# Two attentions of one layer on shared buffers, the second one's first pairs prepared beside the first one's last chunks

## The chip, the cores and the metric

The kernel runs on one core of a Trainium2 chip. The metric is the device time of one launch in microseconds (us). The kernel before took 2742.89 us in the median of three runs (2742.8 to 2744.47).

The engines have short names: PE multiplies matrices (PEld is its weight load), DVE, ACT and POOL work element by element, SP issues transfers. PE writes to PSUM[...]; POOL does not touch PSUM here, so DVE and ACT carry results out of it.

## What is computed

A small vision transformer on 128 images: a convolutional tokenizer makes 64 tokens of 256 features per image, then come two layers. The change concerns the first layer, whose two parts are added to the stream `h` one after the other:

```python
# h = h + A(layernorm(h)), per image, G = 8 groups of 32 features
diff = Qg - Kg                                   # every query with every key
attn = relu(einsum('bqkgd,d->bqkg', relu(diff), w_mlp) + b_mlp)
out  = einsum('bqkg,bkdg->bqdg', softmax(attn, axis=2), Vg)
# h = h + B(layernorm(h)), 4 slices of 64 features, E = 4 experts of 2 heads
xn   = normalized(x) * norm_w                    # x is the layernorm of h
gate = softmax(xn @ router_w.T + router_b)
y    = softmax(q @ k.T * scale) @ v              # per slice, expert and head
y    = y @ proj_w.T + proj_b
out  = x + (sum over experts of y * gate) @ out_w.T
```

A is called relu attention here, B expert attention. The second layer (a linear attention and a mixture of experts) follows and is the same in both kernels. All data are float32.

## The kernel before, in words

The stream stays in SBUF as `h2`, 64 rows of two images each, from the tokenizer to the end of expert attention. Both attentions write the order of the work on all engines out by hand: each engine runs its instructions in the order of the program, so a step that waits holds up all that stands behind it on its engine.

**Relu attention** (`relu_attention`, L290) takes 8 blocks of 16 images, and each block in 8 chunks of 8 query tokens: 64 chunks. In a chunk the maxima or differences of every query and key are formed on DVE (`larger`, L517), on POOL with a relu on ACT (`difference`, L525 and L526), and on ACT alone (`by_query`, L535). PE adds them up (`add`, L327). One chunk later come the softmax (`less_max` L551 to L553, `exponents` L558, `sums` L561, `weights` L565) and the transposes to `at` (L574, L582). The next block's statistics, normalization, transposes, keys and values are spread over the chunks through a table: `at(n, place, step)` puts a step into chunk `n` at one of the places O, X, A, V1, Y, B, W, V2, C, Z, in this order through the chunk. A finished block's sum with the values (`outcome`, L471), its copies (L482), the transposes back (`back`, L489) and the addition to the stream (`added`, L499) stand in chunks 9 to 11 after the block's first. After chunk 63 the last chunk's softmax, the last block's outcome and its addition follow alone; five matmuls without use (L49, `busy`) stand on PE meanwhile.

**Expert attention** (`expert_attention`, L774) opens its own pools after that. It loads its weights, multiplies the value weights with the projection (L806) and the projection's bias with the output weights (L819, `b4`, laid out as `bn`). It works in 16 blocks of 4 rows, called pairs as a row holds two images. A block's steps are the statistics (L843, L844, DVE), `factors` (nine POOL instructions with two powers, L852 to L860), `normal` (POOL: `xn` L866 and the stream with its residual L869), `transpose` and `transposed` (L874, L879), the logits of the router (L885) and their softmax, the gates (L892 to L904), and the gates transposed into `gT` (L908 on PE, L911 on ACT). For the first two blocks and part of the third these steps stand ahead of the first pair (`do("first")`); for the others they are spread over the pairs by a table like the first.

A pair has queries and keys (L933, copied by ACT L937), values (L945: two calls, one for each half of the features; the copies L954 stand on ACT for the first and on DVE for the second), scores (L965), softmax in two halves (L977, L978, L981, L984, L985, and on POOL L991 and L992, which puts the gates into the weights), transposes (L1001, copied by ACT L1004), the sum with the values (`mixed`, L1014, L1022) and the output (L1028). The bias comes in with one more matmul of the transposed gates (L1029), and L1030 adds the result to the stream. Pair p + 1's queries, keys and values and pair p - 1's transposes, sum and output are worked on between pair p's steps.

In PSUM relu attention has 2 banks for sums, 2 for queries, a ring of 3 and one bank for the softmax's transposes; expert attention has 4 banks for scores and a ring of 4.

Of the kernel before, what the change touches and what calls it, by code (L numbers as in the profile page):

```python
# [1 line left out]

# [287 lines left out]
def relu_attention(c, wqkv, wmlp, bmlp):  # L290
# [7 lines left out]
    NP = NB // 2  # L298
    with (
        tc.tile_pool(name="aw", bufs=1) as wp,  # L300
        tc.tile_pool(name="an", bufs=2) as np_,
        tc.tile_pool(name="ab", bufs=2) as bp,
        tc.tile_pool(name="aat", bufs=1) as atp,
# [3 lines left out]
        tc.tile_pool(name="ae", bufs=2) as ep,  # L307
        tc.tile_pool(name="aps", bufs=2, space=PSUM) as pss,
        tc.tile_pool(name="apc", bufs=2, space=PSUM) as psc,
        tc.tile_pool(name="apq", bufs=3, space=PSUM) as psq,  # L310
        tc.tile_pool(name="apt", bufs=1, space=PSUM) as pst,
    ):
        w = wp.tile([P, 2, 3 * D], F32, name="w")
# [21 lines left out]
        class Block:  # L335
# [41 lines left out]
            def transpose(self, i):  # L377

                if i == 0:
                    self.xT = bp.tile([P, 2, NP, P], F32, tag="xT", name="xT")  # L380
                self.ps["x", i] = pt = psq.tile([P, 2, 2, P], F32, tag="pq", name="pt")
                for fc in range(2):
                    for n in range(2):
                        nc.tensor.transpose(
                            pt[:, fc, n], self.xn[:, 2 * i + n, fc * P : fc * P + P], c.ident
                        )
# [5 lines left out]
            def keys(self, s, fo):  # L392

                self.ps["k", s, fo] = pk = psq.tile([P, 8, T], F32, tag="pq", name="pk")
# [15 lines left out]
            def values(self, i):  # L410

                self.ps["v", i] = pv = psq.tile([P, 2, D], F32, tag="pq", name="pv")
# [15 lines left out]
            def key_sums(self):  # L428
                self.ps["b"] = pk = psq.tile([P, T], F32, tag="pq", name="pkb")
# [34 lines left out]
            def outcome(self, hf):  # L464
                self.ps["o", hf] = po = [psq.tile([P, NP, T], F32, tag="pq", name="po") for _ in range(2)]
# [18 lines left out]
            def back(self, i):  # L484

                self.ps["h", i] = pt = psq.tile([P, 2, D], F32, tag="pq", name="pto")
# [14 lines left out]
        class Chunk:  # L501
# [65 lines left out]
            def transpose(self):  # L567


                self.pt = pt = pst.tile([P, 8, 64], F32, tag="pt", name="pt")  # L570
# [50 lines left out]
        for b, x in enumerate(blocks):  # L621
            n = 8 * b

            at(n + 9, "X", of(x.outcome, 0))
            at(n + 9, "A", of(x.outcome_copied, 0, 0))
            at(n + 9, "B", of(x.outcome_copied, 0, 1))
            at(n + 9, "Y", of(x.outcome, 1))
            at(n + 9, "C", of(x.outcome_copied, 1, 0))
            at(n + 10, "O", of(x.outcome_copied, 1, 1))
            for i in range(4):  # L630
                at(n + 10 + i // 2, "XY"[i % 2], of(x.back, i))
                at(n + 10 + (i + 1) // 2, ("V2", "V1")[i % 2], of(x.added, i))
# [48 lines left out]
            at(n, "B", of(x.valued, 3))  # L681

# [4 lines left out]
        with tc.manual_schedule():  # L687
# [61 lines left out]
            old.exponents()  # L749
            old.sums()  # L750
            old.weights()
            c.busy(psq.tile([P, 8, T], F32, tag="pq", name="idle"), blocks[-1].k[:, 0, 0:8], 5)
            old.transpose()
            old.transposed()
            for n in range(len(seq), len(seq) + 12):
                for place in ("O", "X", "A", "V1", "Y", "B", "V2", "C", "Z"):
                    do(n, place)
        assert not work


def expert_attention(c, hd, normw, wr, br, wqkv, wvT, wproj, bproj, wout):
# [7 lines left out]
    with (  # L769
        tc.tile_pool(name="fw", bufs=1) as wp,  # L770
        tc.tile_pool(name="fb", bufs=3) as bp,
        tc.tile_pool(name="fn", bufs=2) as np_,
        tc.tile_pool(name="fv", bufs=3) as vp,
        tc.tile_pool(name="fe", bufs=4) as ep,  # L774
        tc.tile_pool(name="fps", bufs=2, space=PSUM) as pss,
        tc.tile_pool(name="fpq", bufs=4, space=PSUM) as psq,
    ):
        nw = wp.tile([P, 2], F32, name="nw")
        nc.sync.dma_start(nw, normw)
        wrs = wp.tile([P, 2, 4], F32, name="wrs")  # L780
        nc.sync.dma_start(wrs, wr.rearrange("(c p) e -> p c e", p=P))
        brs = wp.tile([P, 4], F32, name="brs")
        nc.sync.dma_start(brs, br.partition_broadcast(P))
        w = wp.tile([P, 2 * D], F32, name="w")
        bp2 = wp.tile([P, 4], F32, name="bp2")
        for k in range(2):
            nc.sync.dma_start(w[k * 64 : k * 64 + 64, :], wqkv)
            nc.sync.dma_start(bp2[k * 64 : k * 64 + 64, :], bproj)
        wv = wp.tile([32, 8, 64], F32, name="wv")
        nc.scalar.dma_start(wv, wvT)  # L790
        wpj = wp.tile([32, 8, 64], F32, name="wpj")
        nc.scalar.dma_start(wpj, wproj)
        wo = wp.tile([P, 2, D], F32, name="wo")
        nc.scalar.dma_start(wo, wout.rearrange("(c p) n -> p c n", p=P))
        eps = wp.tile([P, NB], F32, name="eps")
        nc.gpsimd.memset(eps, LN_EPS)
        one = wp.tile([P, NB], F32, name="one")
        nc.gpsimd.memset(one, 1.0)


        pv = psq.tile([P, 2, D], F32, tag="pq", name="pwv")
        for k in range(2):
            for e in range(4):
                for h in range(2):
                    r = (e % 2 * 2 + h) * 64
                    nc.tensor.matmul(  # L806
                        pv[k * 64 : k * 64 + 64, e // 2, r : r + 64],
                        wv[:, e * 2 + h, :],
                        wpj[:, e * 2 + h, :],
                        start=True,  # L810
                        stop=True,
                    )
        wvp = wp.tile([P, 2, D], F32, name="wvp")
        nc.vector.tensor_copy(wvp, pv)


        pb = psq.tile([4, D], F32, tag="pq", name="pb")
        for fc in range(2):
            nc.tensor.matmul(pb, bp2, wo[:, fc, :], start=(fc == 0), stop=(fc == 1))  # L819
        b4 = wp.tile([4, D], F32, name="b4")  # L820
        nc.vector.tensor_copy(b4, pb)
        bn = wp.tile([P, NB, D], F32, name="bn")
        nc.gpsimd.memset(bn, 0.0)
        for n in range(NB):
            nc.sync.dma_start(bn[4 * n : 4 * n + 4, n, :], b4)
        gTs = [wp.tile([P, P], F32, name=f"gT{k}") for k in range(3)]
        for gT in gTs:
            nc.gpsimd.memset(gT, 0.0)

        class Block:  # L830
# [4 lines left out]
            def __init__(self, p0):  # L835
                self.p0, self.gT = p0, gTs[p0 // NB % 3]

            def statistics(self, n0):
                if n0 == 0:
                    self.mv = np_.tile([P, NB, 2], F32, tag="mv", name="mv")  # L840
                    self.st = np_.tile([P, NB, 6], F32, tag="st", name="st")
# [20 lines left out]
            def normal(self, n):  # L862
                if n == 0:
                    self.xn = np_.tile([P, NB, D], F32, tag="xn", name="xn")
# [199 lines left out]
        def do(key):  # L1064
            for step in work.pop(key, ()):
                step()
# [989 lines left out]
```

## Time and profile before

| | us |
|---|---|
| median of three runs | 2742.89 |
| the profiled execution's own time | 2744.63 |
| its span, first to last instruction | 2742.5 |
| PE, DVE, ACT, POOL busy in the span | 2598.4, 2027.9, 1623.1, 1633.7 |

The span has a tokenizer until about 181 us, relu attention until about 1098 us with its drain until 1114, expert attention until about 1941, and the second layer after that. The page's 40 slices show these stages (each slice is 68.6 us; a digit is the busy share in tenths):

```profile
PE   7989999999999999799999999999699986999997
DVE  5759999999998989477777777777467776444443
ACT  2228888888888888366656666666355543233332
POOL 3328888888888889656566656553233212454444
PEclk9999999999999999899999999999899998999998
```

The dip in the 17th slice is the change from one attention to the other. PEclk is the share of its clock that TensorE was granted. A busy PE is modelled from pipelined matmuls, so 9 on PE does not say that it is at its peak.

### The profile page before, as it was taken

What the parts mean: (1) busy time and instruction counts of PE and PEld (TensorE: products, weight loads), DVE (VectorE), ACT (ScalarE), POOL (GpSimd) and SP (SyncE); (2) the same over time, 40 slices, a digit from 0 to 9 for tenths busy, and PEclk for the clock granted to TensorE, in tenths of its full rate; (3) what the DMA queues carried; (4) which work ended last, traced back from release to release, by engine and by line L of the source; (5) the groups of instructions that cost most, each with busy time, mean ns of one, the idle gap of its engine ahead of it and who ended that gap; (6) DMA issues with size and microseconds to landing.
All of it is one profiled execution on the core that took longest, in us unless ns stands there. A gap on an engine that the chain in (4) does not pass through costs nothing. (4 is left out here: it accounts for less than half of the span.)

```text
span 2742.5 us, 77026 instructions
## 1 busy us (share of the span) xinstructions
PE 2598.4 (95%) x33309; PEld 1733.3 (63%) x33309; DVE 2027.9 (74%) x3025; ACT 1623.1 (59%) x3414; POOL 1633.7 (60%) x1390
## 2 busy tenths in 40 slices
PE   7989999999999999799999999999699986999997
PEld 4553444444344443588888888888466565888886
DVE  5759999999998989477777777777467776444443
ACT  2228888888888888366656666666355543233332
POOL 3328888888888889656566656553233212454444
PEclk9999999999999999899999999999899998999998
DMA  3000000000000000000000000000333454555554
GB/s 109 32 12 1 2 1 2 2 2 2 1 2 1 2 2 1 12 11 19 11 11 19 11 11 18 11 12 17 96 83 85 100 118 149 179 198 197 184 195 134
DMA packets 138015, 140.83 MB, mean 51 GB/s; under 512 B 107747, under 2 KB 121461, under 8 KB 129984
## 3 DMA queue, kind: packets, MB, share of 16 engines
q1 hardware_dynamic: 126928, 117.95, 14.2%
q0 software_dynamic: 7648, 14.77, 1.7%
q8 instruction: 263, 4.31, 0.6%
q10 hardware_dynamic: 3088, 3.08, 0.4%
q14 instruction: 88, 0.72, 0.1%
HBM read 103.96 MB, written 32.54 MB: 50 GB/s over the span
## 5 line engine op out<-in xcount | busy, mean ns | idle before, releaser
L525 POOL TENSOR_TENSOR m<-q,k 128x1024 f32<-128x1024 f32 x384 | 719.0, 1904 | 31.7 <-PE sc L327 16.3
L517 DVE TENSOR_TENSOR m<-pc,k 128x2048 f32<-128x2048 f32 (+1 forms) x320 | 646.7, 2058 | 0.5 <-ACT q L461 0.5
L327 PE MATMUL sc<-m,wide 128*32 128x512 f32 x4096 | 529.7, 599 | 12.0 <-DVE m L517 7.1
L526 ACT ACTIVATE m<-m 128x1024 f32<-128x1024 f32 x384 | 402.5, 1050 | 5.9 <-POOL m L525 5.4
L327 PEld LDWEIGHTS sc<-m,wide 128*32 128x32 f32 x4096 | 126.6, 109 | 259.6 <-issue 146.2
L535 ACT ACTIVATE m<-k,q 128x64 f32<-128x64 f32 x1024 | 271.0, 339 | 0.8 <-DVE k L408 0.8
L977 DVE TENSOR_REDUCE mx<-sc 128x16 f32<-128x1024 f32 x128 | 156.0, 1219 | 153.2 <-PE sc L965 138.1
L992 POOL TENSOR_TENSOR e<-e,mx 128x1024 f32<-128x1024 f32 x128 | 243.4, 1902 | 10.1 <-POOL mx L991 0.2
L937 ACT COPY qk<-pqk 128x512 f32<-128x512 f32 x256 | 139.0, 604 | 132.2 <-PE pqk L933 132.1
L991 POOL TENSOR_TENSOR mx<-mx,gate 128x16 f32<-128x16 f32 x128 | 27.6, 216 | 314.8 <-ACT z L1022 144.3
L1886 PE MATMUL ph<-xt,w1s 128*128 128x256 f32 x896 | 198.8, 380 | 3.6 <-DVE xt L1877 2.6
L1902 PE MATMUL po<-w2s,hT 128*128 128x256 f32 x896 | 198.0, 379 | 0.0
L1004 ACT COPY pT<-pt 128x512 f32<-128x512 f32 x256 | 138.6, 599 | 99.0 <-PE pt L1001 98.3
L1886 PEld LDWEIGHTS ph<-xt,w1s 128*128 128x128 f32 x896 | 169.8, 190 | 28.2 <-DVE xt L1877 3.2
L1902 PEld LDWEIGHTS po<-w2s,hT 128*128 128x128 f32 x896 | 168.1, 190 | 21.7
L933 PE MATMUL pqk<-xT,w 64*128 64x128 f32 x2048 | 169.6, 289 | 3.7 <-issue 3.5
L978 DVE TENSOR_TENSOR e<-sc,mx 128x1024 f32<-128x1024 f32 x128 | 156.7, 1224 | 4.4
L1920 POOL DMA_INDIRECT out<-y,rout x56 | 56.7, 1013 | 167.8 <-ACT hT L1890 124.8
L933 PEld LDWEIGHTS pqk<-xT,w 64*128 64x128 f32 x2048 | 142.3, 189 | 21.1 <-issue 12.0
L984 DVE TENSOR_REDUCE mx<-e 128x16 f32<-128x1024 f32 x128 | 153.3, 1198 | 2.1 <-ACT e L981 2.0
L1890 ACT ACTIVATE hT<-ph,w1s 128x256 f32<-128x256 f32 x224 | 93.0, 470 | 96.9 <-PE ph L1886 96.9
L1001 PE MATMUL pt<-ident,e 128*128 128x128 f32 x1024 | 141.5, 278 | 5.8 <-POOL e L992 2.8
(308 smaller groups left out, 4958.7 us busy)
## 6 DMA issues: line engine op xcount, KB each, us to landing
w1s<-in_we SPq DMA_DIRECT2D x30, 1028.0 KB, 5.0
w2s<-in_we SPq DMA_DIRECT2D x30, 1024.0 KB, 5.2
hd<-h SPq DMA_DIRECT2D x16, 512.0 KB, 3.4
x<-hd SPq DMA_DIRECT2D x16, 512.0 KB, 5.7
h<-hd SPq DMA_DIRECT2D x4, 2048.0 KB, 12.6
hx<-h SPq DMA_DIRECT2D x4, 2048.0 KB
out<-h SPq DMA_DIRECT2D x4, 2048.0 KB, 20.6
xt<-in_x SPq DMA_DIRECT2D x15, 512.0 KB, 3.5
```

The source lines that it names most:

```text
L327: nc.tensor.matmul(dst[j : j + 32], wide[:, hf, s : s + 32], part, start=start, stop=stop)
L517: nc.vector.tensor_tensor(m, bcast(self.pq[:, hf, i : i + n], 3, T), k, ALU.max)
L525: nc.gpsimd.tensor_tensor(m, bcast(self.q[:, hf, s : s + 2], 3, T), k, ALU.subtract)
L526: nc.scalar.activation(m, m, AF.Relu)
L535: nc.scalar.activation(self.parts[i, hf][:, q], self.blk.k[:, hf, i], AF.Relu, bias=self.q[:, hf, i - NB // 2, q : q + 1], scale=-1.0,)
L933: nc.tensor.matmul(pq[par][:, k, eh, :], w[r, f : f + P], self.xT[r, fc], start=True, stop=True)
L977: nc.vector.tensor_reduce(mx, sc, AX.X, ALU.max)
L978: nc.vector.tensor_sub(e, sc, bcast(mx, 2, T))
L984: nc.vector.tensor_reduce(self.sm[x], self.e[x], AX.X, ALU.add)
L992: nc.gpsimd.tensor_mul(e, e, bcast(sm, 2, T))
L1886: nc.tensor.matmul(ph[:, j], self.w1[:, w0 : w0 + P], self.xt[:, fc], start=(fc == 0), stop=(fc == 1))
L1902: nc.tensor.matmul(po, self.hT[:, f, r * P : r * P + P], self.w2[:, f, :], start=(f == 0), stop=(f == 7))
```

## The change

The two attentions use one set of rings in SBUF and one ring of 4 PSUM banks (`Shared`), and the softmax's transposes of relu attention take a bank of that ring instead of one of their own. `expert_attention` is called first; it makes three small loads and two small fills and returns a table `beside` of steps and a function `rest`. Relu attention puts the steps of `beside` into its own table, at chunks 53 to 63. The weights of expert attention lie in ring slots that relu attention has left, the normalized rows and their transposes in three former tiles of relu attention, queries, keys and values in the slots of its `k` and `v`.

The first two blocks are normalized differently from the others: the factors take turns on DVE and POOL (`factors_in_turns`), and ACT makes `xn`. The last block's outcome and addition and the last chunk's softmax move out of relu attention into `first`, which takes pair 0 without a predecessor beside them.

The bias matmul, `bn`, `gT` and the gates' transposes are gone. The values are made by head instead of by half of the features, 32 matmuls of 128 columns a pair instead of 16 of 256, and the projection's bias is added to the values of the second head as they are copied (on DVE); since an expert's softmax weights add up to its gate, this is the same sum. Values have two buffers instead of three.

```diff
+class Shared:
+    def __init__(self, c, ctx):
...
+        self.np_, self.bp = pool("an", 2), pool("ab", 2)
+        self.atp, self.ep, self.small = pool("aat", 1), pool("ae", 2), pool("as", 1)
+        self.psq = pool("apq", 4, space=PSUM)
...
-        tc.tile_pool(name="apq", bufs=3, space=PSUM) as psq,
-        tc.tile_pool(name="apt", bufs=1, space=PSUM) as pst,
...
+        for (n, place), steps in beside.items():
+            at(n, place, *steps)
...
             old.less_max()
-            old.exponents()
-            old.sums()
-            old.weights()
-            c.busy(psq.tile([P, 8, T], F32, tag="pq", name="idle"), blocks[-1].k[:, 0, 0:8], 5)
-            old.transpose()
-            old.transposed()
-            for n in range(len(seq), len(seq) + 12):
-                for place in ("O", "X", "A", "V1", "Y", "B", "V2", "C", "Z"):
-                    do(n, place)
-        assert not work
+        assert not work, work.keys()
+    return old, blocks[-1]
...
+        def factors_in_turns(self, k):
+            v = nc.vector
+            if k == 0:
+                rs, _, _, _, var = self.factors_tiles()
+                v.tensor_scalar_add(rs, var, LN_EPS)
...
+            if k == 1:
+                nc.gpsimd.tensor_tensor(rs, rs, c.nhalf[:, :NB], ALU.pow)
+            if k == 2:
+                v.tensor_mul(ra, var, rs)
+                v.tensor_mul(ra, ra, rs)
+                v.tensor_scalar_add(ra, ra, LN_EPS)
+            if k == 3:
+                nc.gpsimd.tensor_tensor(ra, ra, c.nhalf[:, :NB], ALU.pow)
+            if k == 4:
+                v.tensor_mul(ra, ra, rs)
+                v.tensor_mul(mr, mean, rs)
+                v.scalar_tensor_tensor(self.nb, mean, -1.0, ra, ALU.mult, ALU.mult)
+                v.tensor_scalar_add(rs, rs, 1.0)
...
+        def normal_scalar(self, n):
...
+            nc.scalar.activation(self.xn[:, n, :], hn, AF.Identity, bias=self.nb[:, i], scale=self.ra[:, i])
...
-            def gates_transpose(self):
-            def gates_transposed(self):
...
+        def values(self, h):
...
+            self.pv[h] = pv = [ps([P, 4, P], "pv") for _ in range(2)]
+            for fc in range(2):
+                for j in range(2):
+                    for eh in range(2):
+                        for par in range(2):
+                            r = slice(par * 64, par * 64 + 64)
+                            nc.tensor.matmul(
+                                pv[par][eh * 64 : eh * 64 + 64, 2 * fc + j, :],
+                                self.xT[r, fc, j * 64 : j * 64 + 64],
+                                wt.vp[r, eh, h * P : h * P + P],
...
+        def values_kept(self, h):
+            pv = self.pv.pop(h)
+            for par in range(2):
+                if h == 0:
+                    nc.scalar.copy(self.v[:, par, 0], pv[par])
+                else:
+                    nc.vector.tensor_add(self.v[:, par, 1], pv[par], bcast(wt.b, 1, 4))
...
-                nc.tensor.matmul(po, self.blk.gT, bn[:, self.n, :], start=False, stop=True)
...
+    x, y, z = blocks[:3]
+    by(53, "V2", x.statistics, 0)
+    by(54, "V2", x.statistics, 2)
+    by(55, "Z", wt.load)
+    for n, place, k in ((55, "V2", 0), (56, "W", 1), (57, "V1", 2), (57, "W", 3), (58, "V1", 4)):
+        by(n, place, x.factors_in_turns, k)
+    by(57, "Z", wt.load_values)
+    for n, place, k in ((58, "C", 0), (58, "C", 1), (59, "A", 2), (59, "B", 3)):
+        by(n, place, x.normal_scalar, k)
+    by(58, "Z", wt.values)
+    by(59, "V1", wt.kept)
+    by(59, "Z", x.transpose, 0)
+    by(60, "A", x.transposed, 0)
+    by(60, "Z", x.transpose, 1)
+    by(61, "O", x.transposed, 1)
+    for k in range(NB):
+        by(61 + k // 2, "W", x.stream, k)
+    by(61, "X", x.logits)
+    by(61, "V2", x.logits_less_max)
+    by(62, "A", x.exponents)
+    by(62, "V1", x.sums)
+    by(62, "W", x.gates)
+    by(61, "Z", pair, "queries_keys", 0)
+    by(62, "O", pair, "queries_keys_copied", 0)
+    by(62, "X", pair, "queries_keys", 1)
+    by(62, "B", pair, "queries_keys_copied", 1)
+    by(62, "Z", pair, "values", 0)
+    by(63, "O", pair, "values_kept", 0)
+    by(63, "X", pair, "values", 1)
+    by(63, "V1", pair, "values_kept", 1)
+    by(59, "V2", y.statistics, 0)
+    by(60, "V2", y.statistics, 2)
+    for n, place, k in ((60, "V2", 0), (61, "W", 1), (62, "V1", 2), (62, "W", 3), (63, "V1", 4)):
+        by(n, place, y.factors_in_turns, k)
+    by(61, "V2", z.statistics, 0)
+    by(62, "V2", z.statistics, 2)
+
+    def first(cur, new, chunk, last):
+        new.queries_keys(0)
+        chunk.exponents()
+        new.queries_keys_copied(0)
+        chunk.sums()
+        chunk.weights()
+        cur.scores()
+        cur.less_max(0)
+        for k in range(2):
+            y.normal_scalar(k)
+        new.queries_keys(1)
+        cur.less_max(1)
+        chunk.transpose()
+        new.queries_keys_copied(1)
+        chunk.transposed()
+        cur.exponents(0)
+        for k in range(2, 4):
+            y.normal_scalar(k)
+        last.outcome(0)
+        cur.exponents(1)
+        last.outcome(1)
+        for par in range(2):
+            last.outcome_copied(0, par)
+        cur.sums(0)
+        cur.weights(0)
+        new.values(0)
+        for par in range(2):
+            last.outcome_copied(1, par)
+        cur.sums(1)
+        cur.weights(1)
+        new.values_kept(0)
+        last.back(0)
+        last.back(1)
+        last.added(0)
+        last.added(1)
+        new.values(1)
+        new.values_kept(1)
+        last.back(2)
+        last.back(3)
+        last.added(2)
+        last.added(3)
+        do((0, "POOL"))
+        do((0, "PE"))
```

## What the change will do, predicted before it ran

> **What bounds the kernel now.** I read the page for the engines' shares, then the busy time by windows to find stages and their limits, then the timeline of the seam between the two first-layer attentions and of four steady pairs, and the groups by shape for prices. The page's chain of waits is of no use here: it ends in a last DMA.
>
> Busy time by windows; columns are window, length, busy us (instructions) of PE, PEld, DVE, ACT, POOL, then granted TensorE clock, DMA share, GB/s.
>
> ```profile
> 1058.39:1070.70 12.31, 12.31 (x110) 4.31 (x106) 12.14 (x11) 10.59 (x25) 12.21 (x8) 1.00 0.00 0
> 1098.40:1113.20 14.80, 10.99 (x314) 7.12 (x314) 5.48 (x15) 3.36 (x6) 1.04 (x1) 1.00 0.01 3
> 1113.20:1128.30 15.10, 6.79 (x46) 4.17 (x46) 5.45 (x21) 1.37 (x2) 14.55 (x24) 0.64 0.19 44
> 1128.30:1139.00 10.70, 10.70 (x80) 8.47 (x80) 0.88 (x5) 3.29 (x7) 10.23 (x14) 0.56 0.01 3
> 1351.26:1400.88 49.62, 49.41 (x1139) 41.74 (x1138) 38.90 (x57) 30.96 (x57) 30.16 (x35) 1.00 0.05 14
> ```
>
> The first row is a late chunk of relu attention with nothing extra beside it: DVE (12.14 of 12.31) and POOL (12.21) are both full, so anything put there on either costs time. The next three are the seam: the last chunk drains, then POOL alone prepares pair 0 (14.55 of 15.10), and the clock is granted at 0.64 and 0.56. The last is four pairs of expert attention: PE full (49.41), DVE 38.90.
>
> The timeline of the seam, then of one steady pair:
>
> ```profile
> 1123.29 2.42 POOL L866 TENSOR_SCALAR xn<-h,mv,ra 128x256 f32<-128x256 f32 x2
> ...
> 1139.00 1.60 PE L965 MATMUL sc<-qk 32*64 32x64 f32 x128
> ...
> 1150.26 1.60 PE L965 MATMUL sc<-qk 32*64 32x64 f32 x128
> ...
> 1210.69 1.22 DVE L954 COPY v<-pv 128x512 f32<-128x512 f32 x2
> 1210.73 0.59 PE L1029 MATMUL po<-bn,gT 128*128 128x256 f32 x2
> ```
>
> The last chunk's sums end at 1098.4. Pair 0's scores begin at 1139.0, pair 1's at 1150.26, from where the steady rhythm runs: the seam is 1150.26 - 1098.4 = 51.9 us. Prices, groups by shape (busy, mean ns):
>
> ```profile
> L945 PE MATMUL pv<-wvp,xT 64*64 64x256 f32 x2048 | 142.8, 390 | 0.8 <-ACT qk L937 0.7
> L1014 PE MATMUL pz<-pT,v 128*64 128x64 f32 x4096 | 134.2, 224 | 0.3 <-ACT pT L1004 0.3
> L1029 PE MATMUL po<-bn,gT 128*128 128x256 f32 x128 | 38.1, 379 | 0.0
> ```
>
> Matmuls overlap, so a price on PE is the distance from one group's start to the next group's start, not a mean duration.
>
> **The steady pairs.** Four pairs' scores start at 1351.26, 1363.44, 1376.57, 1388.94, 1400.88: 12.18, 13.13, 12.37, 11.94 us, called A, B, C, D. A and B have statistics on DVE; A and D end with L874's transposes (D with L908 too), B with the logits (1.70), C has the gate softmax. The common part by starts: scores 1.53, queries and keys 1.09 + 1.34, transposes 1.02 + 0.97, L1014 2.01, values 2.03, output 0.97, L1029 0.43 = 11.39.
> - Removed: L1029, 0.43 in each pair; L908 0.11 in D, with its copy on ACT (0.25), which stands beside PE.
> - Added: the values are split by head, so L945's 32 passes of 256 columns become 64 of 128. The streamed columns stay 32 x 256 / 4 tiles = 2048. Before they took 1.89 unstalled and 2.03 with a wait for L1022's copy. At L1001's and L933's 128-column rates (0.97 to 1.09 per 1024) they take 1.94 to 2.18. I take +0.10, hidden to 0.03-0.07 where a wait stood already (C, D); ends 0 and +0.25. A rule speaks against this edit: the Trainium skill, "TensorE: Matmul & The Clock Gate", section "LDWEIGHTS (loading the stationary operand)", prices a load at its columns over 1.2, so 64 columns are 53 ns; 64 loads in series would be 3.4 us, +1.4 a pair, and the change a loss. The trace has 64 loads of 64 columns in L1014 and they pass in 2.01, 31 ns each, in two tiles whose loads evidently overlap; four tiles should not be worse. I take the row.
> - The DVE copy of the second half becomes an add of a bias row: L1224 has that kind at 0.69 for 128x512 against the 0.66 mean of L954's copies on DVE. Nothing, with DVE at 78%.
> - Where the freed time is not kept: in A the statistics push DVE's L954 to 1210.69-1211.9, 11.5 after the scores, and the second half of the next L1001 waits for its PSUM slot. PE already waits there (1.09 for 0.97, L874 0.67 for 0.44), so A keeps 0.05 of its 0.43.
> Per four pairs: A 0.05, B 0.36, C 0.40, D 0.47 = 1.28. Some 15.5 fours: 20 us. With +0.25 for the values it is 0.75 a four, 12 us; with 0, 1.6 and 25.
>
> **The seam.** Gone from it: statistics, factors, normalization, transposes, weights' loads, the product of the value weights and pair 0's queries, keys and values. They now stand beside chunks 53 to 63. What they cost there, by engine and chunk, with rows of before:
> - DVE: 12 rows of statistics at 0.53 (L347 with L348 by starts), 6.3; two sets of factors, 8 small ones of 0.16-0.2 each, 2.7; kept 0.69; gate softmax 0.9; the values' add 1.3. Together 12.
> - POOL: four powers of 1.01, four stream updates of 1.23, gates 0.21: 9.1, of which 3.4 and 3.6 fall in chunks 61 and 62.
> - ACT: four normals 1.6, two xT copies 1.4, exponents 0.2, six copies of PSUM 3.3: 6.5, against 1.7 free in a bare chunk (10.59 of 12.31).
> - PE: transposes 1.1, weights' product about 1, logits 1.7, queries and keys 2.2, values 2: at most 2.8 in one chunk (61), where POOL has 3.4 more.
> Chunks add like the longest engine: the chunk with 1.36 of L499 on DVE took 13.51, the bare ones 12.31. Chunks 53 and 55 last about 14.65 for PE's key and value work, so DVE has 2.3 to spare there. By chunk from 53: 0, 0.4, 0, 0.3, 0.3, 0.75, 1.7, 1.25, 3.4, 3.6, 2.0 = 13.7; I take 14. Ends: 9, if POOL's excess hides DVE's; 21, if DVE's 12 and POOL's 9 come one after the other.
> The waits this adds: the weights' product on PE in chunk 58 waits for two loads issued on SP a chunk (12 us) ahead, where small loads land in 2.0 to 4.1; behind it queues only the chunk's last sum. The logits in 61 wait for ACT's copy early in the same chunk; behind them queue the chunk's sums, at most 0.7. SP has nothing else to do until the first store of hd. Three small loads (0.35-0.47 each on SP) now stand ahead of relu attention's weights at 181; those are first used at 190.2, and a 512 KB load lands in 3.5, so 0, at most 1.3.
> What is left is `first`. Ends counted from the last sum, with the seam's own durations (0.63 exponents, 0.9 sums, 1.04 weights, 1.15 transposes, 0.59 copy, 1.5 for each outcome) and the orders of each engine: less-max 1.7, exponents 2.4, sums 3.4, POOL weights 4.9, the chunk's transposes 6.1, copy 6.8, outcome 8.3 and 9.7, four oT copies until 12.0 (ACT first has pair 0's exponents), back and added in two halves with pair 1's values between, until 16.7, y's transpose and pair 0's first transposes until 17.0; then pair 1's scores. DVE alone has 14.4 in it (less-max 1.7 + 4.9, sums 0.9 + 2.9, L499 2.7, values 1.3). I take 17; ends 15 and 21. A second rule: the Trainium skill, same page, "Part 1: The HAM clock gate", says that PE idle for a window of about 3.4 us falls to half clock. The seam rows of 0.64 and 0.56 agree. In `first` my list leaves PE no hole over 2 us, so I take full clock; at half clock its 11 us of matmuls would reach the 21.
> Seam: 51.9 - 14 - 17 = 21 (ends 28 and 10).
>
> **Sum.** 21 + 20 = 41. The profiled execution took 2744.6 (span 2742.5, 2.1 around it): 2703.6. It stands 1.7 above the median 2742.9, so 2702 as a median. Later stages and the tokenizer are untouched.
>
> **Rivals.**
> 1. Preparation costs more: chunk additions in series, 21, and `first` 21. Seam 10, sum 30: 2713. For it: DVE and POOL are both full. Against: the chunk with L499 paid only its own engine. 19 in 100.
> 2. The freed PE time becomes waits in B, C and D as in A (PSUM slots held by DVE's values). Seam alone plus L908: 2720. Against: in C and D DVE's last values are freed 0.4-0.6 before PE comes. 12.
> 3. Better: preparation 9, `first` 15, values +0: seam 28, steady 24: 2691. 14.
> 4. Slower: the value matmuls become bound by their weight loads. At the rule's 3.4 us all pairs lose 1.4: 64 x 1.4 = 90 against 41 and the 6 counted for it, 2785. It decides from 0.7-0.8 us more per pair, 43 ns a load; L1014's 31 speaks against. 3.
> 5. It does not do what it says, or all gains are given back: 2. The instruction order of the changed program has no matmul of bn, and pair 0's queries stand between chunk 61's sums, so this is unlikely.
> The likeliest case has 50: 2694 to 2710.
>
> Changes within 0.2% (5 us) can't be told from none. Faster 0.95 (likeliest and 1 to 3), same 0.02, slower 0.03. The range 2689 to 2722 takes in 1 to 3 and leaves out their outer ends.
>
> **What would show it.** Seam: from the last chunk's sum to pair 1's scores about 17, clock near 1.00 there, chunks 61 and 62 near 15.8. Pairs: fours of 48.3, the value group 2.05-2.15 by starts, A still 12.1. If the value group takes over 2.5, the rule on loads holds and rival 4 comes near; if C and D keep their 12.37 and 11.94, rival 2; if chunks 58 to 63 grow by over 18, rival 1.

## The result, and the profile after

The changed kernel takes 2725.06 us (median of 4 runs, 2724.27 to 2726.24) against 2742.85 (4 runs, 2742.14 to 2744.47): ratio 0.9935, 95% interval 0.9917 to 0.9952. It is faster, as forecast, but by 17.8 us where 41 were forecast, and 3 us above the range's upper end. The profiled execution took 2724.3, its span is 2722.6.

Busy time by windows of the kernel after, with the columns of the prediction's table. The first two rows are late chunks of relu attention, from one chunk's maximum (L564 on DVE) to the next one's: 59 to 60, and 61 to 62. The third is `first`, from the last chunk's maximum to pair 1's scores. The last is four pairs that nothing disturbed (25 to 28; pairs 17 to 20, which the row of before shows, took 50.47).

```profile
1060.34:1074.93 14.59, 12.52 (x115) 4.84 (x107) 14.31 (x18) 11.79 (x27) 12.24 (x8) 1.00 0.01 1
...
1090.52:1109.90 19.38, 14.94 (x158) 6.18 (x154) 13.99 (x19) 13.01 (x32) 15.76 (x12) 1.00 0.01 2
1125.83:1144.57 18.74, 15.07 (x540) 12.98 (x541) 13.73 (x19) 11.41 (x20) 8.56 (x14) 0.91 0.01 3
...
1440.05:1488.30 48.25, 47.70 (x1257) 42.20 (x1256) 38.74 (x57) 30.69 (x56) 29.56 (x35) 1.00 0.05 15
```

In the first row DVE is busy for 14.31 of 14.59, as the prediction assumed of all these chunks. In the row of 19.38 nobody is full: POOL has 15.76, PE 14.94. That chunk is not long because of one engine's work; engines wait for each other in it. `first` took 18.74 at a clock of 0.91, and four undisturbed pairs take 1.37 less than the 49.62 of before.

Where the time went, by the starts of the same steps in the two profiled executions (minus is earlier or saved):

| from, to | forecast | measured |
|---|---|---|
| relu attention up to chunk 53 | 0 | -0.9 |
| preparation beside chunks 53 to 63 | +14 | +28.3 |
| `first`, in place of the old seam of 51.9 | 17 | 18.7 |
| so the seam | -21 | -4.8 |
| pair 1 to pair 63 | -20 | -18.0 |
| pair 63 to the last scatter of the experts | 0 | +1.4 |
| last scatter to the end | 0 | +2.3 |
| sum | -41 | -20.0 |

(The two profiled executions lie 20.4 apart and the medians 17.8, since the profiled one of before was slower than each of its timed runs.)

The +28.3 by intervals between the maxima of successive chunks, after less before: 0.4 from 53 to 56, then 2.56 (56 to 57), 6.79 (57 to 58), 1.59, 1.67, 3.28, 7.07 (61 to 62) and 4.90. Two places stand out, and the timeline shows why. First DVE and POOL in chunks 57 and 58; start, duration, instruction, and in brackets the idle time before it with its releaser:

```profile
1009.07 5.62 POOL L538 TENSOR_TENSOR m<-q,k 128x1024 f32<-128x1024 f32 x3
...
1011.25 1.59 DVE L902 TENSOR_TENSOR rs<-mv,rs 128x4 f32<-128x4 f32 x1
1012.88 1.83 DVE L903 TENSOR_TENSOR rs<-rs 128x4 f32<-128x4 f32 x1
...
1018.10 1.04 POOL L578 TENSOR_TENSOR e<-e,mx 128x512 f32<-128x512 f32 x1 [3.42 <-DVE mx L575]
...
1020.08 11.21 POOL L538 TENSOR_TENSOR m<-q,k 128x1024 f32<-128x1024 f32 x6
...
1027.06 0.52 DVE L908 TENSOR_TENSOR rs<-rs 128x4 f32<-128x4 f32 x1
1027.51 1.93 DVE L909 TENSOR_TENSOR mr<-mv,rs 128x4 f32<-128x4 f32 x1
1029.37 1.94 DVE L910 SCALAR_TENSOR_TENSOR mr<-mv,rs 128x4 f32<-128x4 f32 x1
```

Products of four numbers per partition take 1.6 to 1.9 us, the time of one GpSimd difference (L538, 5.62 for three). L903 ends at 1014.71, where GpSimd's third difference ends at 1014.69. Then GpSimd itself waits 3.42 us for sums that DVE had not got to. The second place is chunk 62:

```profile
1094.99 0.17 DVE L964 TENSOR_REDUCE gm<-gate 128x4 f32<-128x16 f32 x1 [2.77 <-ACT gate L961]
...
1099.06 1.04 POOL L578 TENSOR_TENSOR e<-e,mx 128x512 f32<-128x512 f32 x1 [3.62 <-ACT m L539]
1100.09 2.43 POOL L927 TENSOR_SCALAR h<-h,rs,mr 128x256 f32<-128x256 f32 x2
1102.48 0.22 POOL L968 TENSOR_TENSOR gate<-gate,gm 128x16 f32<-128x16 f32 x1
1102.65 1.03 POOL L906 TENSOR_TENSOR rs<-rs,nhalf 128x4 f32<-128x4 f32 x1
...
1105.59 1.06 ACT L539 ACTIVATE m<-m 128x1024 f32<-128x1024 f32 x1 [5.71 <-POOL m L538]
```

DVE stands 2.77 us for the gates' exponents on ScalarE (L961), GpSimd 3.62 ahead of the weights, and after that three added steps of GpSimd (L927, L968, L906) delay its next difference, for which ScalarE waits 5.71. (The page names ScalarE's L539 as what released L578. The sums on DVE, L575, ended at 1098.9, just before it, and are the more likely cause.)

### The profile page after: what moved, and what is told of

Read it like the earlier page. It is cut to its first block, busy times and chain, and to the rows that moved or that the text cites. A ratio compares the mean times of both kernels' runs of the same rounds, so it can differ in the third digit from the quotient of the medians.

```text
span 2722.6 us, 80812 instructions
## 1 busy us (share of the span) xinstructions
PE 2569.5 (94%) x35199; PEld 1743.8 (64%) x35199; DVE 2037.2 (75%) x3040; ACT 1623.0 (60%) x3406; POOL 1619.7 (59%) x1364
## 5 line engine op out<-in xcount | busy, mean ns | idle before, releaser
L538 POOL TENSOR_TENSOR m<-q,k 128x1024 f32<-128x1024 f32 x384 | 718.7, 1903 | 31.6 <-PE sc L340 16.1
L539 ACT ACTIVATE m<-m 128x1024 f32<-128x1024 f32 x384 | 402.7, 1050 | 24.7 <-POOL m L538 24.1
L997 ACT COPY kr<-pqk 128x512 f32<-128x512 f32 x256 | 139.1, 604 | 134.2 <-PE pqk L991 134.1
L2084 ACT ACTIVATE y<-y,gf 128x256 f32<-128x256 f32 x56 | 28.0, 507 | 195.8 <-issue 107.1
L1054 ACT ACTIVATE e<-e 128x1024 f32<-128x1024 f32 x128 | 139.5, 1090 | 2.4 <-DVE e L1051 2.2
```

Of the source, the lines that this page charges most:

```text
L538: nc.gpsimd.tensor_tensor(m, bcast(self.q[:, hf, s : s + 2], 3, T), k, ALU.subtract)
L539: nc.scalar.activation(m, m, AF.Relu)
```

## The experiments

My theory after the traces: the second part of the change (bias in the values) gives what was forecast, and the new seam gives nearly nothing, because (a) VectorE's small operations are held while GpSimd runs, and (b) in chunks 62 and 63 waits chain up. The main rival: DVE and POOL were both full, so the added work simply lies in series. Each kernel is compared with the kernel before on its own chip.

**e4_bias and e8_seam: which part gives what.** e4_bias is the kernel before with the second part alone; its core:

```diff
-                    copy = nc.scalar.copy if fc == 0 else nc.vector.tensor_copy
-                    copy(self.v[:, 2 * fc + par], pv[par])
+                    if h == 0:
+                        nc.scalar.copy(self.v[:, par, 0], pv[par])
+                    else:
+                        nc.vector.tensor_add(self.v[:, par, 1], pv[par], bcast(bv, 1, 4))
...
-                nc.tensor.matmul(po, self.blk.gT, bn[:, self.n, :], start=False, stop=True)
-            at(n, "PE", x.gates_transpose)
-            at(n + 1, "ACT", x.gates_transposed)
```

> The kernel before with only the second part of the change: values split by head, the bias added to the second half in VectorE's copy, no bias matmul and no transpose of the gates. The seam stays as it was, 51.9 us. If the steady term is what the traces of the two kernels show (18.0 us from pair 1 to pair 63): 2723 to 2726, about what the whole change gives. If the shared rings or the new places of the copies took part in it: 2727 to 2735. By the forecast's own term of 20: 2723.

2724.74 against 2744.71: 20.0 less (ratio 0.9926, 0.9912 to 0.9939). From pair 1 to pair 63 it is 20.2 faster than before, the seam is unchanged.

e8_seam is the changed kernel with these lines undone and with two fills by GpSimd in `first`, for the bias rows and the gates.

> The changed kernel without its second part: values in 256 columns copied as before, the bias matmul and the transposes of the gates back at their old places (the bias rows are zeros here, so the bias is left out of the result, not out of the work). If the parts add as e4_bias (20.0 us saved) and the whole (17.8) say: 2740 to 2746, no gain from the seam. By the trace of the whole (pair 1's scores 5.7 us earlier, 2 to 4 lost at the end): 2738 to 2742. By the forecast's seam of 21: 2722.

2745.15 (13 runs) against 2745.56 (17 runs): ratio 0.9998, 0.9990 to 1.0006. The new seam by itself gains nothing that can be measured. In its profile pair 1's scores come 2.3 earlier, and the last scatter 2.5 later than before. That profile is not the new seam at its best: its `first` takes 23.3, with the fills and the gates' transposes in it and a clock of 0.85, and it is the slowest of the 13 runs. But the medians say the same without it: the second part alone saves 20.0, the whole change 17.8. So the whole gain of the change is its second part.

**e1_factors, e2_stream, e3_both: what makes the preparation dear.** In e1_factors one operand of each product goes through a spare corner of a PSUM tile that is there anyway; e2_stream takes GpSimd's stream updates of pair 0's block out of the chunks.

```diff
-                v.tensor_mul(ra, var, rs)
-                v.tensor_mul(ra, ra, rs)
+                r = sh.spare(0)
+                v.tensor_copy(r, rs)
+                v.tensor_mul(ra, var, r)
+                v.tensor_mul(ra, ra, r)
```

```diff
-    for k in range(NB):
-        by(61 + k // 2, "W", x.stream, k)
...
         chunk.weights()
+        for k in range(NB):
+            x.stream(k)
```

> The changed kernel, in which each small VectorE operation of factors_in_turns that reads two SBUF operands reads one of them from a spare corner of PSUM instead (three small copies more for each set). Theory: those operations (1.6 to 1.9 us each in chunks 57, 58 and 63, 0.16 to 0.2 for their like) are held until GpSimd's running instruction ends; with a PSUM operand they take 0.2, the growth of chunks 56 to 58 falls from 9.4 us to 1 or 2, and the whole goes from 2725 to 2715 to 2718. Rival (VectorE and GpSimd are both full, and preparation adds in series whatever its form, or the growth comes from ScalarE's normals or the weights' loads): the growth stays above 7 us, 2723 to 2727.

> The changed kernel with the four GpSimd stream updates of pair 0's block taken out of chunks 61 and 62 and put behind the last chunk's weights, where GpSimd was idle for 5.4 us. Theory: in chunks 61 and 62 GpSimd's steps stand ahead of its own last difference, and ScalarE and TensorE wait down that chain; without 2 x 1.22 us a chunk the growth of 61 to 63 falls from 12.0 us to 5 to 7, and `first` stays at 18.7: 2718 to 2721. Rival (the growth there comes from TensorE's queries, keys and logits and from ScalarE's copies of PSUM): growth above 10, 2723 to 2726.

> Both edits together. Theory: the two costs lie in different chunks and add: 2708 to 2713, all chunks from 53 growing by 11 to 15 us in sum. Rival (one full engine hides what the other gives back): no better than the better of the two alone, 2716 to 2720.

The added time by groups of intervals, after less before, for these and the later kernels, with the medians:

| kernel | 56-58 | 58-61 | 61-63 | 53-63 | `first` | median, less before |
|---|---|---|---|---|---|---|
| changed | 9.4 | 6.5 | 12.0 | 28.3 | 18.7 | 2725.06, -17.8 |
| e1_factors | 3.9 | 6.6 | 12.1 | 23.0 | 17.3 | 2717.55, -27.2 |
| e2_stream | 9.4 | 4.8 | 8.3 | 22.9 | 17.4 | 2718.93, -25.8 |
| e3_both | 3.9 | 4.8 | 10.0 | 19.1 | 17.6 | 2717.46, -27.3 |
| e5_gates | 9.8 | 6.5 | 11.6 | 28.4 | 18.7 | 2725.63, -19.9 |
| e9_two | 9.4 | 4.8 | 8.7 | 23.2 | 17.4 | 2720.40, -22.2 |
| e6_three | 1.8 | 5.3 | 3.9 | 11.4 | 17.0 | 2708.33, -37.2 |
| e10_pad | 1.8 | 4.6 | 3.9 | 10.7 | 18.8 | 2704.98, -37.6 |
| e11_stats | 1.8 | 2.3 | 3.8 | 8.0 | 18.6 | 2704.51, -38.1 |
| e12_all | 1.8 | 2.3 | 5.4 | 9.5 | 17.0 | 2701.22, -43.8 |

In e1_factors the same products at the same place took 0.16, with GpSimd's six differences running beside them. The growth of 56 to 58 fell to 3.9, not to the 1 or 2 expected, and what was left of it had a reason of its own. Timeline of POOL and DVE in chunk 58 of e1_factors:

```profile
1019.92 11.21 POOL L541 TENSOR_TENSOR m<-q,k 128x1024 f32<-128x1024 f32 x6
...
1026.90 0.15 DVE L915 COPY pc<-rs 128x4 f32<-128x4 f32 x1
1027.16 0.17 DVE L916 TENSOR_TENSOR pc<-rs,pc 128x4 f32<-128x4 f32 x1
...
1027.51 0.15 DVE L919 SCALAR_TENSOR_TENSOR mr<-mv,pc 128x4 f32<-128x4 f32 x1
1027.58 1.72 DVE L920 TENSOR_SCALAR rs<-rs 128x4 f32<-128x4 f32 x1
```

The last operation adds a number to an SBUF tile and writes to SBUF, and it is held too (1.72; its like in chunk 57 1.04). I had taken this form to be free. So the theory holds, and was too narrow. e2_stream came out at the median expected, but with 8.3 left in the intervals 61 to 63 where 5 to 7 were expected; `first` got 1.3 shorter. e3_both missed: 19.1 of growth, not 11 to 15, and its median is in the rival's range, no better than that of e1_factors. Something else held the intervals 61 to 63; in e3_both's trace DVE still stands 2.71 us for the gates' exponents there.

**e5_gates, e9_two, e6_three: the waits in chunks 62 and 63.** The third suspect is DVE's wait of 2.77. e5_gates puts two steps later; e9_two adds e2_stream's edit; e6_three has these and the factors through PSUM, now with the number forms too.

```diff
-    by(62, "V1", x.sums)
-    by(62, "W", x.gates)
+    by(62, "V2", x.sums)
+    by(63, "W", x.gates)
```

```diff
-                v.tensor_scalar_add(rs, rs, 1.0)
+                v.tensor_scalar_add(rs, r, 1.0)
```

> The changed kernel with two steps of pair 0's gate softmax put later: its sums from VectorE's first place in chunk 62 to its second, its gates from chunk 62 to 63 on GpSimd. Theory: in chunk 62 VectorE stood 2.77 us waiting for ScalarE's exponents of the gates, issued one place ahead, and GpSimd (for the sums), TensorE and ScalarE hang behind it; the interval 61 to 62 falls from 7.07 us over before to 4 to 5, the whole to 2721 to 2723. Rival (GpSimd's steps ahead of its differences set that interval): 61 to 62 stays above 6.3 and the whole at 2724 to 2726.

> The changed kernel with e2_stream's and e5_gates' edits, the factors left as they are. Theory: in chunks 62 and 63 two chains end almost together, VectorE's wait for the gates' exponents and GpSimd's steps ahead of its differences, so that each edit alone took little (1.0 and 0.4 us off the interval 61 to 62) and both take more than their sum: the interval falls from 7.07 us over before to 2 to 3.5; 56 to 58 keeps its 9.4; the whole 2713 to 2717. Rival (what e6_three gained there came from the factors' last operations): the interval stays above 5 and the whole at 2718 to 2722.

> The three edits together (factors through PSUM, now also the three operations with a number for their second operand, whose like took 1.04 and 1.72 us in e1_factors; the stream updates behind the last chunk; the gate softmax later). Theory: growth of 56 to 58 below 2 us (3.9 in e3_both), 61 to 63 at 6 to 7.5 (10.0), the growth from chunk 53 in all 12 to 14.5, near the forecast's 13.7; the whole 3 to 6 us under e3_both, 2711 to 2715. Rival (what is left is the work itself on full engines): within 2 us of e3_both, 2716 to 2719.

e5_gates alone gains nothing: the interval 61 to 62 stayed at 6.7, and the median is in the rival's range. The traces show a reason that neither theory nor rival named. In the changed kernel the products of the second set of factors stand behind the gates' sums, where GpSimd's differences are just ending (at 1095.44); in e5_gates they come first, beside the differences, and are held. The changed kernel, then e5_gates:

```profile
1095.29 0.18 DVE L902 TENSOR_TENSOR rs<-mv,rs 128x4 f32<-128x4 f32 x1
...
1095.50 0.16 DVE L903 TENSOR_TENSOR rs<-rs 128x4 f32<-128x4 f32 x1
```

```profile
1092.69 1.47 DVE L902 TENSOR_TENSOR rs<-mv,rs 128x4 f32<-128x4 f32 x1
...
1094.20 1.82 DVE L903 TENSOR_TENSOR rs<-rs 128x4 f32<-128x4 f32 x1
```

So 3.3 us of hold took the place of 2.77 us of waiting, and the chunk's own sums came hardly sooner: 7.3 us after its maximum, 7.5 in the changed kernel. In e9_two the two products take 0.75 and 1.82. Its theory failed: its intervals 61 to 63 come to 8.7 against the 8.3 of e2_stream alone, and its median is in the rival's range. (Its interval 61 to 62 is 4.06 against 6.10 in e2_stream, but the latter holds 3.4 us at half clock, see e12_all below.) The two waits that stand in parallel on DVE in chunk 62 are those for the gates and for GpSimd: e3_both keeps the first, e9_two the second. e6_three has neither, the interval is 1.98, and the chunks cost 11.4 us in sum, less than expected and less than the forecast's 13.7. What the number forms and the later gates each give in it was not tested. The same stretch of chunk 62 in e6_three:

```profile
1087.77 1.04 POOL L581 TENSOR_TENSOR e<-e,mx 128x512 f32<-128x512 f32 x1 [1.35 <-ACT q L477]
1088.77 1.01 POOL L913 TENSOR_TENSOR rs<-rs,nhalf 128x4 f32<-128x4 f32 x1
...
1091.68 1.06 ACT L542 ACTIVATE m<-m 128x1024 f32<-128x1024 f32 x1
```

GpSimd waits 1.35 instead of 3.62, and ScalarE's next relu no longer waits at all.

**e7_small: the hold by itself.** Two small operations, repeated in 18 early chunks, away from the seam.

```diff
+    def two():
+        nc.vector.tensor_mul(tr, ta, tb)
+    def single():
+        nc.vector.tensor_scalar_add(tr, ta, 1.0)
+    def bank():
+        nc.vector.tensor_mul(sh.spare(0), ta, tb)
+    for n0, f in ((17, two), (25, single), (33, bank)):
+        for n in range(n0, n0 + 6):
+            by(n, "V1", f)
+            by(n, "V1", f)
```

> The changed kernel with two small VectorE operations of 128x4 (their results are not used) more in each of 18 early chunks, beside GpSimd's differences: in chunks 17 to 22 a product of two SBUF tiles, in 25 to 30 an SBUF tile plus a number into SBUF, in 33 to 38 a product of two SBUF tiles into PSUM. Theory (VectorE's SBUF port is held while GpSimd runs, for an operation with two SBUF operands, or with one if its result goes to SBUF too): first and second group 1 to 1.9 us each, their chunks 2 to 3.5 longer. For the third group the theory leaves two cases: two SBUF operands alone hold it (1 to 1.9 each), or it is free (0.2 each, chunks 0.4 longer). Rival (only two SBUF operands are held): second group 0.2 each. Rival 2 (the operations were long in the seam only for what stood around them there): all groups 0.2 each, chunks 0.4 longer.

The three lines by source; after the count, the shortest, median and longest in ns:

```profile
L1167 DVE TENSOR_TENSOR t<-t,t x12: 149/843/1914, 447.9 to 531.2; 128x4 f32<-128x4 f32 x12
L1170 DVE TENSOR_SCALAR t<-t x12: 170/1134/1946, 573.5 to 655.0; 128x4 f32<-128x4 f32 x12
L1173 DVE TENSOR_TENSOR pc<-t,t x12: 170/1029/1946, 696.3 to 779.7; 128x4 f32<-128x4 f32 x12
```

All three are held, and from the chunk ahead of each group to the one behind it the time grew by 11.8, 10.2 and 11.2 us, 1.7 to 2.0 for each of the six chunks, just under what I expected. (The first and the third group hold times at half clock, of which more below; the second holds none.) Both rivals fall. (This is one run, and its chunks are compared with the profiled ones of before.) In 12 of the 18 pairs the second operation passed in 0.16 or 0.17, in 11 of them after the first had been held; so a hold ends with GpSimd's instruction, and what follows on at once may slip through. Where the result goes doesn't matter for two SBUF operands (third group); one operand in PSUM frees it (e1_factors, 0.16).

This agrees with the Trainium skill, "SBUF — State Buffer", section "Who interferes with whom": VectorE and GpSimd share a second pair of SBUF ports; a VectorE instruction with two SBUF inputs meets a GpSimd instruction that reads SBUF there, and an operation with a number can enter a mode that uses the pair; whichever comes first keeps it for its whole instruction. The runs show that these forms are held until a GpSimd instruction ends, and that one operand in PSUM frees them; the ports, the mode and the case in which VectorE comes first are not shown here.

**e11_stats, e10_pad, e12_all: what is left.** e11_stats moves the statistics into earlier chunks, where DVE has room beside PE's key and value work; e10_pad adds 29 small GpSimd memsets at the program's start to e6_three; e12_all has both.

```diff
-    by(53, "V2", x.statistics, 0)
-    by(54, "V2", x.statistics, 2)
+    for n, b, k in ((44, x, 0), (45, x, 2), (47, y, 0), (52, y, 2), (53, z, 0), (55, z, 2)):
+        by(n, "V2", b.statistics, k)
...
-    by(59, "V2", y.statistics, 0)
-    by(60, "V2", y.statistics, 2)
...
-    by(61, "V2", z.statistics, 0)
-    by(62, "V2", z.statistics, 2)
```

```diff
+        for _ in range(29):
+            tc.nc.gpsimd.memset(pad, 0.0)
```

> e6_three with the statistics of the three blocks moved from chunks 53, 54 and 59 to 62 to 44, 45, 47, 52, 53 and 55, where TensorE's key and value work makes chunks of 14.6 us and VectorE has some 2 us free. Theory (VectorE full in the late chunks, their 1.1 to 1.2 us each paid there): the growth from chunk 53 falls from 11.4 us to 6 to 8.5, the early chunks stay within 0.5 of before, the whole 2704 to 2707. Rival (GpSimd's and ScalarE's added steps pay the late chunks anyway): growth 10 or more, 2707 to 2709.

> e6_three with 29 small GpSimd memsets ahead of everything, so that GpSimd issues as many instructions as in the kernel before. In all kernels with the new seam the time from the last scatter to the end of the span is 2.1 to 2.4 us longer, in a gap of GpSimd ahead of its last drain. If the gap goes with GpSimd's place in its program: it goes away, 2 us under e6_three or, if the memsets delay the tokenizer by their 2 to 3 us, level with it. If it goes with the new seam otherwise: the gap stays at 2.5, and the time is level or up to 3 us longer.

> e11_stats with e10_pad's 29 memsets. If the two savings add (3.4 and 2.2 to 3.3 us from e6_three): 2701 to 2703, 40 to 42 us under before, and 11.8 us from the last scatter to the end. If what e10_pad saved beside the gap (1 us in the second layer) was chance: 2702 to 2704.

e11_stats: growth 8.0, as expected, and no early chunk is longer by more than 0.1; 2704.51. e10_pad: 2704.98, and its gap at the end is gone: from the last scatter to the end 11.85 us, as in the kernel before, against 14.08 in e6_three. By the medians neither can be told from e6_three: they are 38.1 and 37.6 below before on their chip, e6_three 37.2 on its own. e12_all: 2701.22, ratio 0.9838 (0.9824 to 0.9851), 43.8 below before; it is faster than both kernels of this case. Its interval 62 to 63 grew by 3.73, in e11_stats by 2.21, and its `first` took 17.0 instead of 18.6. Windows of that interval and of `first` in e11_stats, then in e12_all:

```profile
1093.63:1106.87 13.24, 10.87 (x130) 4.11 (x124) 9.73 (x17) 9.78 (x24) 7.88 (x6) 1.00 0.00 1
1106.87:1125.49 18.62, 15.08 (x540) 13.00 (x540) 13.72 (x19) 11.41 (x20) 13.43 (x18) 0.91 0.02 4
```

```profile
1094.11:1108.87 14.76, 12.40 (x130) 4.66 (x124) 9.73 (x17) 9.78 (x24) 7.88 (x6) 0.88 0.00 1
1108.87:1125.87 17.00, 13.75 (x540) 11.84 (x540) 13.72 (x19) 11.41 (x20) 12.44 (x15) 1.00 0.01 4
```

The two stretches hold the same matmuls, and together they last 31.86 and 31.76. A time of 3.4 us at half clock lies in `first` in the one execution and in the interval ahead of it in the other. Such times lie in single intervals of most of these kernels, so a difference under 2 us in one interval is not to be read from one trace.

## Why the prediction was wrong

**The steady pairs: right, but for one thing.** The forecast of 20 is what e4_bias gives (20.0 by medians, 20.2 by pairs). In the changed kernel it is 18.0, in the later kernels that have both parts 13.4 to 17.4 in their profiled executions. An undisturbed four is 48.25 (forecast 48.3). The value group costs nothing: median 2.03 before, 2.04 after from start to start, so 64 loads of 64 columns pass in 32 ns each. The row of L1014 was the right one to take; the 53 ns a load of the Trainium skill ("TensorE: Matmul & The Clock Gate", "LDWEIGHTS (loading the stationary operand)") do not add up in series over four tiles. What the forecast had no term for are idle spells of PE, mostly inside a group of scores, where PE waits for nothing that the profile's releasers show: four of 1.0 to 1.4 us in the changed kernel, four of 0.8 to 1.3 in e4_bias, seven in e2_stream, one of 0.9 before. The record of transfers has something: ahead of the longest, which ends at 1354.10, the only transfer from 1351 on is a load of instructions.

```profile
q8 instruction: 1, 0.02, 2.7%
```

Of the 66 spells over 0.8 us in these pairs of all fourteen kernels, 63 begin within 2 us of the start of such a load (a random moment does so 4 times in 10), and PE goes on 1.1 to 1.7 us after the load is in. So PE very likely waits for instructions; no run here changes the loads to prove it. There are 139 of them in pairs 1 to 63 before and 152 or 153 with the values made by head. Rival 2 did not happen.

**The preparation: the step that failed.** "two sets of factors, 8 small ones of 0.16-0.2 each, 2.7" priced them by the durations of small operations that GpSimd does not hold. They take up to 1.95, and all sixteen 13.4 us in the changed kernel; their like in e6_three take 3.8. For chunks 57 and 58, the intervals 56 to 58, the forecast had 1.05, and 9.4 was measured. Of this e1_factors gives back 5.5, and e6_three, with the number forms too, 7.5, while the small operations in it fall from 8.1 to 4.0 and 1.6; the rest goes with a time at half clock that the changed kernel has in the interval 57 to 58 and these two have not. The trace of before had the nearer row. It is in the groups by shape of the kernel before, an operation with the same operands beside the same differences:

```profile
L362 DVE SCALAR_TENSOR_TENSOR nb<-mv,rs 128x4 f32<-128x4 f32 x14 | 14.8, 1055 | 1.1 <-POOL rs L358 1.1
```

Its mean is 1055 ns. At that price the five products of each set, ten in all, are 10.6 us instead of some 1.8; they took 10.4. For the number forms that trace gave no warning: L357, an SBUF tile plus a number, has 125 ns there.

The second failed term is "chunks add like the longest engine". It held where the added work was plain (58 to 61: 1.6, 1.7 and 3.3 for 1.7, 1.25 and 3.4). In 61 to 63, which is chunks 62 and 63, it gave 5.6, and 12.0 was measured, with no engine full. The forecast listed which queues stand behind the weights' product and the logits; it did not ask what stands behind DVE's sums of the gates (2.77 of waiting for ScalarE), nor behind GpSimd's steps, which come ahead of its own difference (5.71 for ScalarE). With these three causes taken away the chunks grow by 11.4 against 13.7, but four stream updates (4.9 us of GpSimd) then stand in `first`; chunks and `first` together are 28.4 in e6_three against the forecast's 31. The excess of 14.6 is thus accounted for in sum: e6_three gives back 16.9. How it splits among the three is not, since they hide each other.

**`first`: mis-sized, by the clock.** 18.7 for 17, at 0.91 where full clock was assumed, because PE was to have no hole over 2 us. Its longest is 2.2 us, and PE is busy for 1.23 of the 3.41 us up to 1137.10; in the next 3.41 the clock is halved:

```profile
1133.69:1137.10 3.41, 1.23 (x118) 1.07 (x109) 3.11 (x5) 2.39 (x4) 1.30 (x2) 0.99 0.00 0
1137.10:1140.52 3.42, 3.42 (x63) 2.92 (x51) 0.02 (x1) 2.13 (x4) 3.26 (x5) 0.51 0.02 5
```

So a shorter hole was enough than the idle window of about 3.4 us that the prediction went by. `first` took 17.0 to 17.6 in the six kernels of the table that had full clock in it and 18.6 to 18.8 in the others, and e6_three and e10_pad, the same here, stand on either side. In the six, pair 1 then takes 1.3 to 2.4 longer than in e4_bias, with one of the idle spells in it, so little of this is won.

**Later stages untouched: not quite.** 1.4 was lost in the second layer and 2.3 behind its last scatter. The first has the clock in it. Windows of the same stretch of linear attention, before, then after:

```profile
2192.00:2204.00 12.00, 10.68 (x117) 7.70 (x112) 4.41 (x10) 2.97 (x4) 3.76 (x2) 1.00 1.01 174
```

```profile
2168.00:2180.00 12.00, 11.09 (x101) 7.42 (x96) 3.93 (x9) 2.97 (x4) 3.42 (x2) 0.86 1.03 176
```

The granted clock is 0.86 where it was 1.00 (0.83 in the 10 us after it), and 2.2 us are lost there, of which some was won elsewhere. The six executions with such times of half clock at this place (changed, e6_three, e7_small, e9_two, e11_stats, e12_all) lose 0.5 to 1.8 in the second layer; six without them (e1_factors to e5_gates, and e10_pad) lose 0.0 to 0.4. So it goes with the clock; what brings it about is not shown. e8_seam loses 3.9, and why is open.

**The rivals.** Rival 1 (dearer preparation, 2713) had the right place and direction, for it set 21 + 21 where 28.3 + 18.7 were measured, but its reason, engines' work in series, was not the cause: e6_three does the same work for 11.4 + 17.0. None of the others came.

## What to carry to other kernels

Price a small operation by its row beside the same neighbour, not by its size: where GpSimd runs long instructions, a VectorE operation with two SBUF operands, or an SBUF tile and a number, costs up to one GpSimd instruction, and one operand in PSUM makes it cheap again. A step moved into a full pipeline costs its own time only if what it waits for is long done and nothing urgent is queued behind it; otherwise ask that of each such step on every engine, and expect that taking away one of two waits in the same place shows nothing (e5_gates: the hold stepped in for the wait) until the other is gone. And measure the parts of a change apart: here one part gave all, the other nothing until it was mended, and then 19 (e6_three) to 26 us (e12_all, with the memsets) more than the change as it was.

## What the runs showed of the hardware that was not expected

The last scatters of the changed kernel and of e10_pad on GpSimd, whose spans are 2722.6 and 2700.6:

```profile
2708.42 1.00 POOL L2097 DMA_INDIRECT out<-y,rout  x1 [0.30 <-issue]
```

```profile
2688.80 1.00 POOL L2107 DMA_INDIRECT out<-y,rout  x1 [0.30 <-issue]
```

From the start of that scatter to the end are 14.1 us in the first (also in e6_three, e11_stats, e9_two: 13.9 to 14.1) and 11.85 in the second, as in before. The difference is a gap of 2.4 to 2.7 us on GpSimd, ahead of its last drain, in place of 0.37. It goes with how many instructions GpSimd has issued: the kernels with 2043 or 2045 of them in the trace have it and those with 2072 or 2071 don't, and 29 memsets that compute nothing took it away (e10_pad, e12_all). The record of transfers has a load of instructions in it. From 2712.84 to 2715.51, the gap in the changed kernel, the only transfer is:

```profile
q14 instruction: 1, 0.01, 1.3%
```

All kernels with the gap have this load 5.3 to 5.5 us after the start of the scatter, and the last drain starts 1.0 to 1.2 us after it is in. With PE's spells above this makes a wait for instructions likely on two engines. That the queue is GpSimd's own, no run shows.
